# Layer 3's offsets and modulation: computed once per image and copied to all partitions through memory, for six of eight images

## The chip, the cores and the metric

The kernel runs on one core of one Trainium2 chip. The core has five engines that each run their own instruction stream in order and wait for one another by semaphores: TensorE (PE in the profile; its weight loads are PEld), VectorE (DVE), ScalarE (ACT), GpSimd (POOL) and SyncE (SP), which here only issues DMAs. Data live in HBM ("DRAM" in the code), in SBUF (128 partitions) and in PSUM, where TensorE writes its results. The metric is the device time of one execution in microseconds (us); lower is better.

## The reference

Eight images of 384 channels and 32x32 pixels in float32 pass four residual layers, each after a group norm. Layer 0 is a convolutional attention, layer 1 a mixture of four two-layer experts, layer 2 a ternary depthwise and pointwise convolution, layer 3 a deformable attention. The change lies in layer 3:

```python
q = einsum('bchw,oc->bohw', x, q_w)
q_off = q.reshape(B * 3, 128, H, W)                      # three groups
off = conv(q_off, dw_w, stride 2, pad 2, depthwise 5x5)  # 16x16 positions
off = gelu(batchnorm(off + dw_b))
om = einsum('bchw,oc->bohw', off, pw_w)                  # 3 numbers per position
offset, modulation = om[:, 0:2], sigmoid(om[:, 2:3])
pos = tanh(offset) * (2 / 16) + reference_points         # (y, x)
x_s = bilinear_sample(x, pos) * sigmoid(modulation)
k, v = kv_w @ x_s                                        # 256 keys per image
out = x + proj_w @ softmax(q k / 8) v + proj_b
```

So each image has 3 x 768 numbers `om`: for each of three groups and 256 positions a y offset, an x offset and a modulation. All channels of a group share them.

## The kernel before, in words

Layer 0 runs first over all images. Then layers 1, 2 and 3 run image by image. Layer 1 is cut into 48 *units* per image (`layer1`): 24 `hidden` units (six matmul records `ph` each, line L1244) and 24 `result` units (six records `y` each, L1265). In the main loop the layers 2 and 3 of image b (`layers(b)`, a generator) are written out together with the units of layer 1 of image b+1. The generator's `yield` gives a number, the idle time that TensorE is supposed to have there; the loop adds it to `due` and writes out one unit for every `UNIT = 2.6` of it. Units left over when the image ends are written out at the end. The last two images take another way: image 6 runs up to `yield None` with the units of image 7, and then its remainder is interleaved with image 7.

The framework orders each engine's instructions by this written order but puts later work that is ready ahead of work that isn't, by its own model of durations. So the order in the trace is near to the written one, not equal to it.

Around the change, layer 3 of an image does this:

- `pq`, `px` (L1384, L1407): q, and the transposed image `xT` which the sampling needs.
- `off` (L1452, L1454): the 5x5 convolution on VectorE, 25 taps; then Gelu on ScalarE (L1459).
- `pom` (L1467, L1468): three matmul pairs, one for each of y offset, x offset and modulation. The weight `pw3` in memory holds each of the three vectors repeated in 128 columns, so that the result of each pair stands in all 128 partitions at once. A Tanh (L1471) takes each pair from PSUM into the tile `om0`, `om1` or `om2`, each 128 x 768. The modulation's is scaled by 0.5, as a sigmoid is computed through a tanh.
- VectorE turns the offsets into pixel positions (L1477, L1481); ScalarE finishes the modulation (L1482; L1483 on VectorE) and the x weights (L1485, L1486); for each of eight row blocks ScalarE (L1499, L1500) and GpSimd (L1501) make the sampling weights `wt`, and TensorE samples with them (`xsb`, L1505).
- `xs` (L1512), `pk`, `pv` (L1519, L1528), attention (`s` L1545, `p` L1552, `pav` L1561, `pss` L1587), projection `pf` (L1650), output.

The pool `flat` has five buffers, `om0` to `om2` one each. SyncE's DMA queue carries, per image, three stores of layer 2's result (L1355), three loads of x (L171) and three of layer 0's output (L1179) for a later image, and three stores of the output (L1661).

```python
            for idle in this:
                ...
                due += idle
                while due >= UNIT and units:
                    units.pop(0)()
                    due -= UNIT
```

Of the kernel before, what the change touches and what calls it, by code (L numbers as in the profile page):

```python
# [7 lines left out]
F32 = mybir.dt.float32  # L8
AF = mybir.ActivationFunctionType
# [3 lines left out]
B, C, H, W = 8, 384, 32, 32  # L13
N = H * W
P = 128
# [17 lines left out]
NPAIR3, HS, LS, NG = 3, 16, 256, 3  # L33
# [19 lines left out]
def tile_kernel(ctx: ExitStack, tc: tile.TileContext, i: dict, out: bass.AP):  # L53
    nc = tc.nc
# [4 lines left out]
    dram = ctx.enter_context(tc.tile_pool(name="dram", bufs=1, space=bass.MemoryType.DRAM))  # L59
# [7 lines left out]
    def bank(name):  # L67
        return ps_mm.tile([P, HALF], F32, tag="mm", name=name)
# [150 lines left out]
    with ExitStack() as pa:  # L219
# [10 lines left out]
        for s in range(2):  # L230
            t = wa.tile([P, KC, H + 2, W], F32, name=f"pad{s}")
# [122 lines left out]
        for n, (b, g) in enumerate(work):  # L354
# [6 lines left out]
            if n in todo:  # L361
                f, b2 = todo.pop(n)
# [10 lines left out]
            for h, k in steps:  # L373
                dx, c0, c1, o0 = TAPS[k]
                rows = slice(h * (H // 2), (h + 1) * (H // 2))
                if g < NGC:
                    lhs, rhs = cw[:, g, dx, :], st[:, rows, c0:c1]
                else:
                    r = slice(32 * h, 32 * h + 3 * GR)
                    lhs, rhs = cwr[r, dx, :], st[r, rows, c0:c1]  # L380
                nc.tensor.matmul(  # L381
                    pk[h].rearrange("p (h w) -> p h w", w=W)[: 3 * nch, :, o0 : o0 + c1 - c0],
                    lhsT=lhs, rhs=rhs, start=(k == 0), stop=(k == 2),
# [31 lines left out]
        for v in range(3):  # L415
            nc.tensor.matmul(
                pm[:, 0, v, : 2 * (NGC + 1)], lhsT=sel0[:, v, :],
                rhs=both.rearrange("p s g -> p (s g)"), start=True, stop=True,
# [3 lines left out]
                rhs=rest.rearrange("p s k -> p (s k)"), start=True, stop=True,  # L422
# [28 lines left out]
    scale = HD0 ** (-0.5)  # L451
# [40 lines left out]
    with ExitStack() as pb:  # L492
# [17 lines left out]
        for v, nm in enumerate(("wq0", "wk0", "wv0")):  # L510
            t = wb.tile(list(i[nm].shape), F32, name=f"{nm}_sb")
# [225 lines left out]
    _, sco, sho = sc_o  # L737
# [51 lines left out]
    with tc.If(redo > 0):  # L789
        with ExitStack() as pb:  # L790
# [5 lines left out]
            for v, nm in enumerate(("wq0", "wk0", "wv0")):  # L796
                t = wb.tile(list(i[nm].shape), F32, name=f"{nm}_e")
# [6 lines left out]
            with tc.For_i(0, B) as bi:  # L804
                act = []
                for v in range(3):
                    g = work[v]
                    nc.sync.dma_start(
                        out=g, in_=raw[v][bass.ds(bi, 1)].rearrange("o p c n -> p (o c) n")
# [3 lines left out]
                for t in range(NT8):  # L813
                    pv = bank(f"pv_e{t}")
                    for c in range(KC):
                        nc.tensor.matmul(
                            pv[:, :C], lhsT=act[2][:, c, t * P : (t + 1) * P],
                            rhs=w_in[2][:, c, :], start=(c == 0), stop=(c == KC - 1),
# [8 lines left out]
                for v in range(2):  # L827
                    ts = qp.tile([P, NPAIR0, N], F32, tag=f"qk{v}", name=f"qk{v}_e")
                    for pr in range(KC):
                        for h in range(2):  # L830
                            pq = bank(f"pq{v}_e{pr}_{h}")
                            for c in range(KC):
                                nc.tensor.matmul(
                                    pq, lhsT=w_in[v][:, c, pr * P : (pr + 1) * P],
                                    rhs=act[v][:, c, h * HALF : (h + 1) * HALF],
                                    start=(c == 0), stop=(c == KC - 1),
# [8 lines left out]
                for pr in range(NPAIR0):  # L845
                    qt, kt = qks[0][:, pr, :], qks[1][:, pr, :]
                    for h in range(2):
                        pav = bank(f"pav_e{pr}_{h}")
                        for j, r in enumerate(HR):
                            hd = 2 * pr + j  # L850
                            pt = qp.tile([P, NT8, HALF], F32, tag="pt", name=f"pt_e{pr}_{h}_{j}")
                            for qc in range(4):
# [3 lines left out]
                                for kh in range(2):  # L856
# [3 lines left out]
                                        start=True, stop=True,  # L860
# [18 lines left out]
                            for kc in range(NT8):  # L879
                                nc.tensor.matmul(  # L880
                                    pav[64 * j : 64 * j + 64, :],
                                    lhsT=vt[:, kc, 2 * hd : 2 * hd + 2, :].rearrange(
                                        "p a b -> p (a b)"
                                    ),
                                    rhs=pt[:, kc, :],
                                    start=(kc == 0),
                                    stop=(kc == NT8 - 1),
# [5 lines left out]
                for m in range(KC):  # L893
                    for h in range(2):
                        hs = slice(h * HALF, (h + 1) * HALF)
                        po = bank(f"po_e{m}_{h}")
                        for c in range(KC):
                            nc.tensor.matmul(
                                po, lhsT=wo0[:, c, m * P : (m + 1) * P], rhs=att[:, c, hs],
                                start=(c == 0), stop=(c == KC - 1),  # L900
# [3 lines left out]
                    out=o_dram[bass.ds(bi, 1)].rearrange("o p c n -> p (o c) n"), in_=oe  # L904
# [19 lines left out]
    def load_w(name):  # L924
        src = i[name]
        t = wd.tile(list(src.shape), F32, tag=name, name=name + "_sb")
        nc.sync.dma_start(out=t, in_=src)
        return t
# [27 lines left out]
    pl = Pools(pd, "d")  # L956
# [190 lines left out]


    x2_dram = dram.tile([B, P, KC, N], F32, name="x2")
    NU3 = 2 * NPAIR3  # L1150
    rec3 = wd.tile([P, B * NU3, 16], F32, name="rec3")
    bad3 = wd.tile([P, 1], mybir.dt.int32, name="bad3")
# [205 lines left out]
    def layer3(pl, b, xt, put, general):  # L1358
# [14 lines left out]
        else:  # L1373
            t = pl.img(f"h3_{b}")
# [5 lines left out]
        for m in range(KC):  # L1380
            whole, pq = pair(last, f"pq3_{b}_{m}")
            for h in range(2):
                for c in range(KC):
                    nc.tensor.matmul(  # L1384
                        pq[h], lhsT=wq3[:, c, m * P : (m + 1) * P], rhs=h3[h][:, c, :],
                        start=(c == 0), stop=(c == KC - 1),
# [11 lines left out]
        else:  # L1398
            t = pl.img(f"xT_{b}").rearrange("p c n -> p (c n)")
# [38 lines left out]
        for t in (12, *range(12), *range(13, 25)):  # L1438
# [4 lines left out]
            for g in gs:  # L1443
                if g is None:
                    d = off.rearrange("p g h w -> p (g h) w")[:, :, c0 : c1 + 1]
                    f = q.rearrange("p g (h w) -> p (g h) w", h=H)[:, dy : : 2, :]
                else:
                    d = off[:, g, r0 : r1 + 1, c0 : c1 + 1]
                    f = src[:, g, 2 * r0 + dy : 2 * r1 + dy + 1 : 2, :]
                f = f[:, :, 2 * c0 + dx : 2 * c1 + dx + 1 : 2]  # L1450
# [7 lines left out]
        offf = off.rearrange("p g h w -> p (g h w)")  # L1458
# [3 lines left out]
        yield None  # L1462

        om = []
        for r in range(3):
            po = big(f"pom_{b}_{r}")
            nc.tensor.matmul(po[:, :512], lhsT=pw3[:, r, :], rhs=offf[:, :512], start=True, stop=True)  # L1467
            nc.tensor.matmul(po[:, 512:768], lhsT=pw3[:, r, :], rhs=offf[:, 512:], start=True, stop=True)  # L1468
            t = pl.one([P, NG * LS], f"om{r}", f"om{r}_{b}")

            nc.scalar.activation(t, po[:, : NG * LS], AF.Tanh, scale=1.0 if r < 2 else 0.5)  # L1471
            om.append(t)
            yield 0.3
# [21 lines left out]
        for t in range(NT8):  # L1495
# [8 lines left out]
            for g in range(NG):  # L1504
                nc.tensor.matmul(  # L1505
                    xps[g][:, sl], lhsT=xT[t // T2][:, t % T2, g * P : (g + 1) * P], rhs=wt[:, g, :],
                    start=False, stop=(t == NT8 - 1), skip_group_check=True,
# [9 lines left out]
        for m in range(NPAIR3):  # L1517
            for c in range(KC):
                nc.tensor.matmul(  # L1519
                    pk[:, m * LS : (m + 1) * LS], lhsT=wk3[:, c, m * P : (m + 1) * P],  # L1520
                    rhs=xs[:, c, :], start=(c == 0), stop=(c == KC - 1),
# [4 lines left out]
        for t in range(2):  # L1526
            for c in range(KC):
                nc.tensor.matmul(  # L1528
                    pv[:, t, :C], lhsT=xs[:, c, t * P : (t + 1) * P], rhs=wv3[:, c, :],
                    start=(c == 0), stop=(c == KC - 1),  # L1530
# [40 lines left out]
        if not general:  # L1571
            ps = scores(*units[0])
            for u, (pr, h) in enumerate(units):
# [5 lines left out]
                nc.vector.transpose(tu.rearrange("p a b -> p (a b)"), pav)  # L1579
                if u + 1 < NU3:  # L1580
                    ps = scores(*units[u + 1])
# [4 lines left out]
                for j in range(2):  # L1586
                    nc.tensor.matmul(  # L1587
                        pss[64 * j : 64 * j + 64, :], lhsT=ones[:, :64],
                        rhs=p01[:, j * HALF : (j + 1) * HALF], start=True, stop=True,
                    )  # L1590
                tss = blocks("ts")
                nc.vector.transpose(tss.rearrange("p a b -> p (a b)"), pss)
                rc = rec3[:, b * NU3 + u, :]
                nc.vector.reciprocal(rc, tss[:, :, 0])
# [8 lines left out]
        else:  # L1603
            for pr, h in units:
                pav = vbank(f"pav3_{b}_{pr}_{h}")
                for j in range(2):
                    r = slice(64 * j, 64 * j + 64)
                    nm = f"3_{b}_{pr}_{h}_{j}"
                    s = big(f"s{nm}").rearrange("p (a k) -> p a k", a=4)
                    for qc in range(4):  # L1610
# [3 lines left out]
                            start=True, stop=True,  # L1614
# [6 lines left out]
                    for qc in range(4):  # L1621
                        nc.scalar.activation(
                            p[:, qc, :], s[:, qc, :], AF.Exp, bias=mx[:, qc : qc + 1],
                            scale=0.125, accum_out=rs[:, qc : qc + 1],
# [14 lines left out]
                    for kc in range(2):  # L1639
                        nc.tensor.matmul(  # L1640
                            pav[r, :], lhsT=vt[:, kc, hd * 64 : (hd + 1) * 64], rhs=pt[:, kc, :],
                            start=(kc == 0), stop=(kc == 1),
                        )
                nc.vector.tensor_copy(att[:, pr, h * HALF : (h + 1) * HALF], pav)
        for m in range(KC):
            pf = big(f"pf_{b}_{m}")
            for h in range(2):
                hs = slice(h * HALF, (h + 1) * HALF)
                for pr in range(NPAIR3):
                    nc.tensor.matmul(  # L1650
                        pf[:, hs], lhsT=wp3[:, pr, m * P : (m + 1) * P], rhs=att[:, pr, hs],
                        start=(pr == 0), stop=(pr == NPAIR3 - 1),
# [16 lines left out]
    for b in range(1, B):  # L1669
        logits(b)  # L1670
        del fetched[b, 0]
        for n in (2, 3) if b == 1 else (b + 2,):
            if n < B:
                fetch_next(n)
        if b + 3 == B:
            w2, b2 = load_w("w2"), load_w("b2")
            wq3, wk3, wv3, wp3 = (load_w(n) for n in ("wq3", "wk3", "wv3", "wp3"))
            pb3, dw3, bn3, pw3 = (load_w(n) for n in ("pb3", "dw3", "bn3", "pw3"))
            ref3, npos = load_w("ref3"), load_w("npos")
        if b + 1 < B:  # L1680
            for _ in range(3 if b < 6 else 2):
                units.pop(0)()
    route(units, 2 * NE * KC)
    coefficients()
    with pd:
# [30 lines left out]
        for _ in following:  # L1716
            pass
        okt = pl.flat([P, B * NU3 * 16], "okt3")
        recf = rec3.rearrange("p u q -> p (u q)")
# [9 lines left out]
    with tc.If(redo3 > 0):  # L1729
        with ExitStack() as pe:  # L1730
            pl = Pools(pe, "g")
            with tc.For_i(0, B) as bi:
                xt = pl.img("x_g")
                nc.sync.dma_start(
                    out=xt, in_=x2_dram[bass.ds(bi, 1)].rearrange("o p c n -> p (o c) n")
# [28 lines left out]
def _layouts(a):  # L1764
    import numpy as np

    f = np.float32
    L = {}
# [53 lines left out]
    for n in "qk":  # L1822
# [27 lines left out]
    L["bn3"] = np.stack(  # L1850
        [a[f"L3_conv_{n}"] for n in ("dw_b", "bn_w", "bn_b", "bn_mean", "bn_var")], axis=1
    )
    L["pw3"] = np.repeat(a["L3_conv_pw_w"].T[:, :, None], P, axis=2)
    lin = np.linspace(0.5, HS - 0.5, HS, dtype=f) / f(HS) * f(2.0) - f(1.0)
    ref = np.stack([np.repeat(lin, HS), np.tile(lin, HS)])
# [26 lines left out]
```

## Time and profile before

| What | us |
|---|---|
| median of 3 runs (lowest to highest) | 3773.9 (3771.85 to 3775.54) |
| the profiled execution | 3772.12 |
| its span, first to last instruction | 3770.3 |
| TensorE busy in the span | 3647.7 |
| VectorE busy | 1818.9 |
| ScalarE busy | 1316.8 |
| GpSimd busy | 194.8 |
| one image of the main loop (from the end of one `pf` to the next, image 1) | 227.47 |
| TensorE busy in it | 226.00 |
| VectorE busy in it | 135.77 |

The busy times of the page are unions of intervals; a matmul's end is modelled, so TensorE's busy time says only that it had something in work. The distance between the starts of consecutive matmul records says what a record costs. Every float32 matmul of this kernel shows as two records.

### The profile page before, as it was taken

What the parts mean: (1) busy time and instruction counts of PE and PEld (TensorE: products, weight loads), DVE (VectorE), ACT (ScalarE), POOL (GpSimd) and SP (SyncE); (2) the same over time, 40 slices, a digit from 0 to 9 for tenths busy, and PEclk for the clock granted to TensorE, in tenths of its full rate; (3) what the DMA queues carried; (4) which work ended last, traced back from release to release, by engine and by line L of the source; (5) the groups of instructions that cost most, each with busy time, mean ns of one, the idle gap of its engine ahead of it and who ended that gap; (6) DMA issues with size and microseconds to landing.
All of it is one profiled execution on the core that took longest, in us unless ns stands there. A gap on an engine that the chain in (4) does not pass through costs nothing.

```text
span 3770.3 us, 39346 instructions
## 1 busy us (share of the span) xinstructions
PE 3647.7 (97%) x15754; PEld 1521.3 (40%) x15754; DVE 1818.9 (48%) x2841; ACT 1316.8 (35%) x1564; POOL 194.8 (5%) x153
## 2 busy tenths in 40 slices
PE   7999899999999999999799999999999999999898
PEld 3444333333333333333244534445444444444433
DVE  5876223232323232323346557565664666547664
ACT  2222364554545454534222321323222232322222
POOL 0000000000000000000000010200102010010111
PEclk9999999999999999999899999999999999999898
DMA  6777311111212020212340000100001001010000
GB/s 201 240 245 245 107 50 37 65 44 55 61 41 74 25 74 26 72 27 71 138 183 25 26 34 17 34 34 17 34 17 49 19 17 34 17 51 17 1 34 18
DMA packets 83097, 242.64 MB, mean 64 GB/s; under 512 B 18336, under 2 KB 18864, under 8 KB 82520
## 3 DMA queue, kind: packets, MB, share of 16 engines
q1 hardware_dynamic: 69894, 200.56, 16.1%
q10 hardware_dynamic: 13008, 39.43, 3.1%
q8 instruction: 128, 2.10, 0.2%
q14 instruction: 67, 0.55, 0.0%
HBM read 122.78 MB, written 75.50 MB: 53 GB/s over the span
## 4 chain that ended last, share of the span: by engine, by line
PE 40%; DVE 9%; ACT 1%; issue 0%; POOL 0%; DVEq 0%; POOLq 0%; ACTq 0%
PE y L1265 11%; PE ph L1244 8%; DVE y L1339 6%; PE pq L1384 3%; PE pw L1347 3%; PE pf L1650 3%; PE s L1545 3%; PE pav L1561 2%; PE pss L1587 1%; DVE hd L1230 1%; DVE off L1454 1%; PE pk L1519 1%; PE pv L1528 1%; PE xsb L1505 1%; PE plog L1007 1%; PE pom L1467 1%
## 5 line engine op out<-in xcount | busy, mean ns | idle before, releaser
L630 ACT ACTIVATE p<-s 128x1024 f32<-128x1024 f32 x512 | 496.4, 1021 | 496.9 <-PE s L623 496.5
L1265 PE MATMUL y<-hd,w_sb 128*128 128x512 f32 x1080 | 491.0, 600 | 3.6 <-DVE hd L1230 3.6
L638 PE MATMUL pav<-p,vt 64*64 64x512 f32 x4096 | 486.6, 590 | 0.0
L1244 PE MATMUL ph<-h,w_sb 128*128 128x512 f32 x1104 | 483.3, 594 | 0.0
L623 PE MATMUL s<-qk,qk 48*64 48x512 f32 x3072 | 372.7, 600 | 4.4 <-ACT p L630 4.4
L381 PE MATMUL pk<-st,cw_sb 126*126 126x512 f32 x720 | 316.4, 600 | 5.2 <-DVE ga_a L118 4.2
L1244 PEld LDWEIGHTS ph<-h,w_sb 128*128 128x128 f32 x1104 | 207.6, 190 | 253.1 <-issue 250.3
L1265 PEld LDWEIGHTS y<-hd,w_sb 128*128 128x128 f32 x1080 | 199.3, 191 | 249.8 <-issue 236.0
L638 PEld LDWEIGHTS pav<-p,vt 64*64 64x64 f32 x4096 | 156.2, 133 | 285.4 <-issue 285.1
L595 DVE COPY ta<-pav 128x512 f32<-128x512 f32 x64 | 44.3, 691 | 439.2 <-PE pav L638 439.2
L1339 DVE SCALAR_TENSOR_TENSOR y<-h,tap,y 128x992 f32<-128x992 f32 (+1 forms) x192 | 233.8, 1241 | 1.6
L1454 DVE SCALAR_TENSOR_TENSOR off<-q,dw_sb,off 128x225 f32<-128x225 f32 (+3 forms) x432 | 213.3, 549 | 1.7
L1254 ACT ACTIVATE hd<-ph,b_sb 128x512 f32<-128x512 f32 x180 | 122.7, 682 | 258.3 <-PE ph L1244 257.9
L381 PEld LDWEIGHTS pk<-st,cw_sb 126*126 126x126 f32 x720 | 137.6, 193 | 176.8 <-issue 167.8
L623 PEld LDWEIGHTS s<-qk,qk 48*64 48x64 f32 x3072 | 102.5, 132 | 241.5 <-issue 184.6
L78 DVE COPY qk<-pq 128x512 f32<-128x512 f32 x48 | 33.2, 691 | 293.6 <-PE pq L558 281.8
L387 ACT COPY y<-pk 126x512 f32<-126x512 f32 (+1 forms) x136 | 75.9, 584 | 250.7 <-PE pk L381 118.3
L1552 ACT ACTIVATE p<-s 128x1024 f32<-128x1024 f32 x96 | 93.1, 1021 | 173.4 <-PE s L1545 173.3
L575 PE MATMUL po<-att,wo_sb 128*128 128x512 f32 x288 | 135.7, 621 | 8.5 <-DMA att<-al 8.5
L1230 DVE TENSOR_TENSOR hd<-hd,cb 128x512 f32<-128x512 f32 x180 | 122.2, 684 | 35.4 <-ACT hd L1254 35.0
L1347 PE MATMUL pw<-y,upw 128*128 128x512 f32 x288 | 129.7, 603 | 7.6 <-DVE y L1339 7.6
L558 PE MATMUL pq<-g,wq_sb 128*128 128x512 f32 x288 | 132.8, 612 | 2.2 <-ACT g L483 2.2
(278 smaller groups left out, 4004.4 us busy)
## 6 DMA issues: line engine op xcount, KB each, us to landing
g<-raw SPq DMA_DIRECT2D x72, 512.0 KB
st<-pad SPq DMA_DIRECT2D x180, 168.0 KB
raw<-y ACTq DMA_DIRECT2D x180, 168.0 KB
xa<-in_x_dram SPq DMA_DIRECT2D x24, 512.0 KB
xh<-in_x_dram SPq DMA_DIRECT2D x48, 256.0 KB
f<-in_x_dram SPq DMA_DIRECT2D x24, 512.0 KB
f<-o SPq DMA_DIRECT2D x24, 512.0 KB
o<-ot SPq DMA_DIRECT2D x42, 256.0 KB
```

The source lines that it names most:

```text
L381: nc.tensor.matmul(pk[h].rearrange("p (h w) -> p h w", w=W)[: 3 * nch, :, o0 : o0 + c1 - c0], lhsT=lhs, rhs=rhs, start=(k == 0), stop=(k = ...
L558: nc.tensor.matmul(pq, lhsT=w_in[v][:, c, pr * P : (pr + 1) * P], rhs=acts[b][v][:, c, h * HALF : (h + 1) * HALF], start=(c == 0), stop=(c ...
L575: nc.tensor.matmul(po, lhsT=wo0[:, c, m * P : (m + 1) * P], rhs=atts[b][:, c, hs], start=(c == 0), stop=(c == KC - 1),)
L623: nc.tensor.matmul(s[64 * k : 64 * k + 64, j * HALF : (j + 1) * HALF], lhsT=kt[r, k0 : k0 + 64], rhs=qt[r, h * HALF : (h + 1) * HALF], sta ...
L630: nc.scalar.activation(p, s, AF.Exp, scale=scale)
L638: nc.tensor.matmul(pav[k][64 * j : 64 * j + 64, :], lhsT=vts[b % 2][r, kc, 2 * hd : 2 * hd + 2, :].rearrange("p a b -> p (a b)"), rhs=p[r, ...
L1230: nc.vector.tensor_tensor(hd, hd, state["cb"], ALU.mult)
L1244: nc.tensor.matmul(ph, lhsT=w1[:, e, c, dc * P : (dc + 1) * P], rhs=state["h1"][c], start=(c == 0), stop=(c == KC - 1),)
L1265: nc.tensor.matmul(y, lhsT=w2[:, e, dc, m * P : (m + 1) * P], rhs=state[h, k], start=(k == 0), stop=(k == NE * KC - 1),)
L1339: nc.vector.scalar_tensor_tensor(d, f, tap2[:, c, t : t + 1], d, ALU.mult, ALU.add)
L1347: nc.tensor.matmul(pw[h], lhsT=upw2[:, c, m * P : (m + 1) * P], rhs=y[c][:, hs], start=(c == 0), stop=(c == KC - 1),)
L1454: nc.vector.scalar_tensor_tensor(d, f, dw3[:, t : t + 1], d, ALU.mult, ALU.add)
```

## The change

For images 0 to 5 (`b < B - 2`) the three pairs of matmuls become one: the weight is `pw3[:, :, 0]`, three columns, so that the result has three partitions, one for each of y offset, x offset and modulation. One Tanh on those three partitions, with a per-partition scale from a small new constant `half3`, takes it into a `flat` tile. SyncE stores the three rows to a new DRAM tensor `om_dram` and loads each row back into all 128 partitions of `om0`, `om1` and `om2`. A single `yield 7.0` stands in place of three `yield 0.3`. Images 6 and 7, and the general path that is taken only when softmax sums leave their range, keep the three pairs. The constant `half3` is loaded with layer 3's other constants.

```diff
     x2_dram = dram.tile([B, P, KC, N], F32, name="x2")
+    om_dram = dram.tile([B, 3, NG * LS], F32, name="omd")
...
         om = []
-        for r in range(3):
+        if b < B - 2:
+
+            po = big(f"pom_{b}")
+            for k in (slice(0, 512), slice(512, 768)):
+                nc.tensor.matmul(po[:3, k], lhsT=pw3[:, :, 0], rhs=offf[:, k], start=True, stop=True)
+            t = pl.flat([P, NG * LS], f"oms_{b}")
+            nc.scalar.activation(t[:3], po[:3, : NG * LS], AF.Tanh, scale=half3)
+            nc.sync.dma_start(out=om_dram[b], in_=t[:3])
+            for r in range(3):
+                t = pl.one([P, NG * LS], f"om{r}", f"om{r}_{b}")
+                nc.sync.dma_start(out=t, in_=om_dram[b, r : r + 1].to_broadcast([P, NG * LS]))
+                om.append(t)
+            yield 7.0
+        for r in range(0 if om else 3):
             po = big(f"pom_{b}_{r}")
...
-            ref3, npos = load_w("ref3"), load_w("npos")
+            ref3, npos, half3 = load_w("ref3"), load_w("npos"), load_w("half3")
...
+    L["half3"] = np.array([[1.0], [1.0], [0.5]], f)
```

## The prediction

> **What bounds the kernel.** I read the page first, then the windows of one image, then TensorE's timeline around `pom` and at the image's end.
>
> ```profile
> PE 3647.7 (97%) x15754; PEld 1521.3 (40%) x15754; DVE 1818.9 (48%) x2841; ACT 1316.8 (35%) x1564; POOL 194.8 (5%) x153
> ```
>
> ```profile
> 2236.97:2464.44 227.47, 226.00 (x655) 102.10 (x655) 135.77 (x199) 62.51 (x85) 20.11 (x16) 1.00 0.08 28
> ```
>
> TensorE has work in 226.00 of an image's 227.47 us; it waits 1.5 us. So a TensorE microsecond removed from a main-loop image is one off the time, if the waits don't grow.
>
> ```profile
> 2141.76 1.02 PE L1467 MATMUL pom<-off,pw_sb 128*128 128x512 f32 x2
> 2142.62 0.59 PE L1468 MATMUL pom<-off,pw_sb 128*128 128x256 f32 x2
> 2143.05 1.02 PE L1467 MATMUL pom<-off,pw_sb 128*128 128x512 f32 x2
> 2143.91 0.59 PE L1468 MATMUL pom<-off,pw_sb 128*128 128x256 f32 x2
> 2144.34 1.02 PE L1467 MATMUL pom<-off,pw_sb 128*128 128x512 f32 x2
> 2145.20 0.59 PE L1468 MATMUL pom<-off,pw_sb 128*128 128x256 f32 x2
> 2145.63 5.31 PE L1244 MATMUL ph<-h,w_sb 128*128 128x512 f32 x12
> 2150.78 2.74 PE L1265 MATMUL y<-hd,w_sb 128*128 128x512 f32 x6
> 2153.35 0.54 PE L1505 MATMUL xsb<-wt,xT 128*128 128x48 f32 x4
> ```
>
> No bracket at a line's end means no wait. Starts give the cost: a pair takes 1.29 us (2141.76 to 2143.05), a unit six records of 0.43, 2.58 us. TensorE runs three units (12 `ph`, 6 `y`) between `pom` and the sampling. What the sampling waits for:
>
> ```profile
> 2143.25 0.81 ACT L1471 ACTIVATE om<-pom 128x768 f32<-128x768 f32 x1 [0.60 <-PE pom L1468]
> 2146.91 0.92 ACT L1482 ACTIVATE om<-om,quarter 128x768 f32<-128x768 f32 x1
> 2147.73 0.92 ACT L1485 ACTIVATE om<-om,npos_sb 128x768 f32<-128x768 f32 x1
> 2148.90 0.83 ACT L1486 ACTIVATE om<-om 128x768 f32<-128x768 f32 x1
> 2149.81 0.49 POOL L1501 TENSOR_TENSOR wt<-wt,om 128x144 f32<-128x144 f32 x1 [68.23 <-ACT om L1486]
> ```
>
> The first `wt` is there at 2150.30, TensorE comes to it at 2153.35: 3 us of slack today.
>
> **What the Trainium skill says.** "TensorE: Matmul & The Clock Gate", Back-to-back issue gap: the gap follows the streamed columns N. So three output rows cost what 128 do per streamed column; the trace agrees, as `pk` with 18x18 weights has 574 ns beside 579 ns with 126x126 (modelled ends, so weak). "DMA: Bandwidth & Descriptors", Two DMAs through the same engine are not ordered: a DMA that reads what another wrote must be issued after a semaphore wait. So SyncE waits for the store before it issues the loads; no DMA pair of that kind near `pom` shows it before. Two prices are below.
>
> **The change part by part.** Clock: t = 0 at the start of `pom`.
>
> *Removed.* Two pairs per image: 2 x 1.29 = 2.58 us of TensorE, on the path. Six images: 15.5 us. Two Tanhs (0.81 us each) leave ScalarE, which is busy 62.5 of 227 us: worth nothing; it is covered by TensorE's work and has slack without it.
>
> *Added: the trip through memory.* Tanh starts at 1.49 as now (2143.25 less 2141.76) and ends at 2.30; ScalarE's cost here goes by the row's 768 elements, which stay. Then store and loads. SyncE is free there: in image 1 it issues its stores from 2295.5 to 2305.3 and the next load at 2389.28, while `pom` starts at 2369.57. Queued behind the four DMAs is only that load of x, whose data are wanted an image later: cost nothing.
>
> The store (9 KB): no row shows one. The page's Anatomy of one DMA section prices a transfer at about 2.0 us plus bytes/436e3, for the GpSimd path; the estimate is 2.0 (bounds 1.5 to 3.0). It lands at 4.4, with 0.1 for semaphores.
>
> The loads (384 KB each): the nearest row is layer 0's output, 512 KB from memory. SyncE issues the first at 2008.68, and VectorE, waiting for it, starts at 2012.32: 3.64 us. The DMA view of image 1 shows 280 GB/s while x is loaded (from 2389), at which 512 KB take 1.87; the fixed part is 1.77. A load of 384 KB takes 1.40 more, and the three share the same DMA engines: `om0` at 4.4 + 1.77 + 1.40 = 7.6, `om1` 9.0, `om2` 10.4. What is new is that 128 reads fetch the same 3 KB. Low bound 0.9 us each (435 GB/s, the page's ceiling): `om2` 8.9. High bound: Latency and other measured facts gives 103 GB/s where streams fall on the same memory channels, 3.8 us each: `om2` 17.6. I take the middle, as the reads are whole rows.
>
> From L1482, which wants `om2`, to the first `wt` today: 2150.30 - 2146.91 = 3.39. VectorE's work on `om1` (0.96 + 0.56) is done at about 10.6, so ScalarE's order keeps this distance: `wt` at 10.4 + 3.4 = 13.8.
>
> *Moved: the cover.* The ledger of yields for a whole image adds up to 118.55; at 2.6 that is 45 of 48 units, three left over. The trace agrees:
>
> ```profile
> 2221.35 15.61 PE L1650 MATMUL pf<-att,wp_sb 128*128 128x512 f32 x36
> 2236.80 7.89 PE L1265 MATMUL y<-hd,w_sb 128*128 128x512 f32 x18
> 2244.53 1.05 PE L1208 MATMUL w<-ident_sb,w 128*128 128x128 f32 x8
> ```
>
> With 7.0 for 0.9 the sum is 124.65, 47 units, one left. Between `pom` and the sampling the yields add up to 7.0 + 6.0 + 2.0 = 15.0 in place of 0.9 + 6.0 + 2.0 = 8.9: stepping the ledger from the image's start writes six units there in place of four. One of them runs ahead of `pom` today, while `pom` waits for Gelu (ten `ph` units stand before `pom`, nine by the ledger); so five remain in place of the three seen. TensorE reaches the sampling at 1.29 + 5 x 2.58 = 14.2, just after `wt` at 13.8. GpSimd's fourth block follows 2.95 later (2153.25 less 2150.30), at 16.8; TensorE wants it at 14.2 + 3 x 0.65 = 16.1, unless a unit lies between. So I count a wait of 0.5 us per image (0 to 0.7). A unit written earlier costs TensorE nothing: the two units leave the end of the image, where they kept TensorE busy after `pf`; there the next image's `ph` follow, whose inputs are ready at 2219.9, well before. VectorE's chain from the last `y` to layer 2's pointwise product starts earlier by what TensorE saves and keeps its length; TensorE waits 0.67 for it at 2290.47 today, and will again.
>
> *VectorE and ScalarE wait in order.* L1477 waits for `om0`; behind it are the `hd` products (L1230) of the two `ph` units, which the second `y` group needs. Both `ph` are done by 6.5, before `om0`, so the products mostly go ahead. If not, three units of `y` don't need them.
>
> *Buffers and constants.* The new `flat` tile lives from 1.5 to 4.4, when one more of five (`off`) is held: nothing waits. `half3` is one more tiny load among fourteen issued from 1912 to 1926: nothing.
>
> Sum: 6 x (-2.58 + 0.5) = -12.5. The profiled execution, 3772.12 with its span of 3770.3, becomes 3759.6; the median lies 1.8 above it, so 3761.4.
>
> **The rivals.**
>
> *The loads are late (slower).* Place: the wait of ScalarE's L1482 and VectorE's L1477 on the loads; TensorE then stands at `xsb`, because order is fixed and no further unit fills. Each microsecond of `om2` after 10.8 costs one per image. It decides at 10.8 + 2.58 = 13.4, where the gain is gone: 3.0 us per load in place of my 1.4, wherever the row is read at under about 160 GB/s (393 KB by 2.4 us, the store as priced). At the high bound `om2` 17.6 gives `wt` at 21.0, a wait of 6.8, net +4.2 per image, +25: 3799. For it: no row in the profile reads one row 128 times. Against it: DMA is at 0.00 of its capacity in this stretch, and the framework can place more `y` there if its model expects long DMAs, as 12 units remain.
>
> *The wait takes most of the gain (no change).* Store plus loads 2 us slower than priced: wait 2 to 2.5, net -0.5 x 6 = -3: 3771.
>
> *More gain.* All lands in time and the moved units also close the 0.55 wait before `pav`: 6 x -2.9 = -17: 3757. Little speaks for it; those waits have units near already.
>
> *It does not do what it says*: if the three-column matmul cost more than a pair of 128 columns. Weights of three columns load no slower; I give it no chance of its own.
>
> **How the numbers follow.** A measurement of this kernel tells about 0.2%, 7.5 us, from no change. In time or a wait up to 1.3 us: 0.50 (predicted; 3756 to 3766 of itself). Wait of 1.3 to 3.8: 0.18. Later: 0.32, of which about half past 3795. With half of them reached and the early end kept, the range is 3755 to 3798; some 0.16 lie above and 0.02 below.
>
> **What would show it.** Two `pom` pairs fewer on TensorE's timeline and `ph` 1.29 after `pom`. The image period: 227.3 less 2.1, about 225.3. The wait of PE `xsb` L1505 on POOL `wt`: absent before, up to 0.7 per image after; over 2.6 the forecast is wrong. Waits of L1477 and L1482 on DMA, and the distance from the store's issue to them, price the trip. After `pf`, 6 `y` records, not 18. The forecast also falls if the framework places `xsb` so early that TensorE stands before it, or if image 6 and 7, not changed, get another order.

## The result and the profile after

| | before | after |
|---|---|---|
| median of four runs (lowest to highest), us | 3772.88 (3765.86 to 3775.54) | 3756.68 (3755.51 to 3758.4) |
| ratio, with its 95% interval | | 0.996 (0.9943 to 0.9978) |
| the profiled execution, us | 3772.12 | 3756.19 |
| its span, us | 3770.3 | 3754.4 |

The change makes the kernel faster by 16.2 us (0.4%). The forecast was 3761.4 with a range of 3755 to 3798: right in direction and within the range, the time 4.7 us lower than foretold. (1.0 us of that is the base: the forecast started from 3773.9, the median of three runs, and the fourth brought it to 3772.88.) Three terms behind it were not what the prediction said.

The page of the kernel after, its line of busy times (engine, busy us, share, instructions):

```profile
PE 3631.3 (97%) x15706; PEld 1507.2 (40%) x15706; DVE 1820.7 (48%) x2841; ACT 1309.6 (35%) x1552; POOL 191.3 (5%) x153
```

TensorE is still busy 97% of the span and is 16.4 us less busy; 48 of its records are gone, which is 6 images x 2 pairs x 4 records. The same stretch of image 1 as was shown before, from the end of one `pf` to the end of the next (window, its length, and then the busy time of PE, PEld, DVE, ACT and POOL, the clock, the DMA share and GB/s):

```profile
2239.40:2463.73 224.33, 222.88 (x648) 99.64 (x646) 135.93 (x199) 61.29 (x83) 19.50 (x16) 1.00 0.09 34
```

The image takes 224.33 in place of 227.47 us, and TensorE's idle remainder is 1.45 as before (1.47). The whole gain of this image is TensorE work that takes less time; no wait came or went in it. TensorE's timeline from `pom` to the sampling, in image 0 as in the lines before the change (start, duration, engine, line, out<-in, weights, tile, records):

```profile
2142.78 1.46 PE L1470 MATMUL pom<-off,pw_sb 128*3 128x512 f32 x4
2144.17 5.42 PE L1245 MATMUL ph<-h,w_sb 128*128 128x512 f32 x12
2149.42 7.89 PE L1266 MATMUL y<-hd,w_sb 128*128 128x512 f32 x18
2157.14 0.54 PE L1519 MATMUL xsb<-wt,xT 128*128 128x48 f32 x4
```

One pair is left. Between it and `xsb` stand 12 `ph` and 18 `y` records, five units where there were three, and no bracket: TensorE doesn't wait for the trip. One pair now takes 1.39 us (2142.78 to 2144.17), not 1.29, and twelve `ph` take 5.25, not 5.15. The trip itself, in three views of the same stretch: SyncE's queue (`omd` is the DRAM tensor `om_dram`, `oms` the tile that is stored), the waiting engines, and the DMA view between 2130 and 2180 in bins of 1.25 us.

```profile
2145.19 0.26 SPq L1473 DMA_DIRECT2D omd<-oms  x1
2146.75 1.27 SPq L1476 DMA_DIRECT2D om<-omd  x3
```

```profile
2144.27 0.89 ACT L1472 ACTIVATE oms<-pom,half_sb 3x768 f32<-3x768 f32 x1 [0.70 <-PE pom L1470]
...
2150.95 0.95 DVE L1491 SCALAR_TENSOR_TENSOR om<-om,ref_sb 128x768 f32<-128x768 f32 x1
...
2153.41 0.92 ACT L1496 ACTIVATE om<-om,quarter 128x768 f32<-128x768 f32 x1
...
2156.22 2.14 POOL L1515 TENSOR_TENSOR wt<-wt,om 128x144 f32<-128x144 f32 x4 [73.69 <-ACT om L1500]
```

```profile
GB/s 0 0 0 0 0 0 0 7 0 0 0 0 7 0 182 300 396 66 0 0 0 0 0 0 0 0 0 0 0 0 0 197 383 419 249 20 3 0 0 0
```

SyncE issues the loads 1.56 us after the store. The bins 182, 300, 396 and 66 hold 1.18 MB (944 GB/s x 1.25 us), which is three loads of 384 KB; at the two full bins' mean rate of 348 GB/s they move from about 2148.1 to 2151.5. The second hump, up to 419, is the load of x. VectorE takes `om0` at 2150.95, right behind an `hd` product, and ScalarE takes `om2` at 2153.41, both without waiting for a DMA. GpSimd starts the four first `wt` blocks 13.44 us after `pom`; the first is ready at about 13.9 (0.5 us later, as one took before), and TensorE arrives at 14.36: the cover holds with 0.4 us to spare.

The end of image 0, on the same timeline:

```profile
2223.95 15.61 PE L1664 MATMUL pf<-att,wp_sb 128*128 128x512 f32 x36
2239.40 2.74 PE L1266 MATMUL y<-hd,w_sb 128*128 128x512 f32 x6
```

One unit is left after `pf`, not three.

**Where the 15.9 us of the span are.** I cut each trace at TensorE's first `pw` record of an image. From the first image's to the seventh's, so over the six changed images, the distance is 1364.13 before and 1344.98 after: -19.15. What lies ahead of it is 0.95 longer, and what lies behind it (images 6 and 7 and the general path) 2.28 longer: 3770.3 - 19.15 + 0.95 + 2.28 = 3754.4. This distance is a steady measure where the total is not: in all twelve profiled executions of this document TensorE's granted clock is 1.00 over it, and two executions of the change give 1344.98 and 1345.03. Ahead of it, where these kernels differ by no more than the load of a small constant, the clock is 0.98 and the stretch takes anything from 2055.9 to 2068.8 us. In the comparisons below, "the six images" is this distance in the profiled execution. Within an image I sum, for each product, the distances from the start of each of its records to the next record of TensorE, whatever that is, so that the sums of all products add up to the image. Between the two kernels they differ, in image 1, in these:

```
us in image 1     before   after
pom                 3.87    1.39
s                  14.82   13.77
ph                 61.97   62.17
y                  64.20   64.46
xsb                 3.45    3.39
all others          equal within 0.01
```

Only the first line was in the forecast. The second is a gain nobody asked for, the third and fourth are costs.

### The profile page after: what moved, and what is told of

Its sections match the earlier page's. It is cut to its first block, busy times and chain, and to the rows that moved or that the text cites. A ratio compares the mean times of both kernels' runs of the same rounds, so it can differ in the third digit from the quotient of the medians.

```text
span 3754.4 us, 39254 instructions
## 1 busy us (share of the span) xinstructions
PE 3631.3 (97%) x15706; PEld 1507.2 (40%) x15706; DVE 1820.7 (48%) x2841; ACT 1309.6 (35%) x1552; POOL 191.3 (5%) x153
```

## The experiments

Three accounts fit the total. The two pairs give the gain, and the rest is chance. Or the new order of the units gives it. Or the trip costs something on other engines that the order makes good. My theory, by the sums of image 1: the pairs give most of it, the shorter `s` comes from the new places of the `result` units, and the trip itself is hidden.

**The yields alone.** Three pairs in 128 partitions as before, no trip; only the ledger as in the change.

```diff
-            yield 0.3
+            yield 6.4 if r == 2 and b < B - 2 else 0.3
```

> The kernel before with the yields of the change alone: the third pair of images 0 to 5 yields 6.4 in place of 0.3, so two units of layer 1 move from behind the projection to ahead of the sampling. All three pairs stay, nothing goes through memory. Theory (the gain is the two pairs of matmuls): TensorE has the same work, so at most the 1.1 to 1.4 us per image that the attention's waits shrank by comes back: 3766 to 3773. Rival (the gain is the new order of units): most of the 16 us, 3757 to 3761.

Measured: 3771.73 (3767.54 to 3773.74), ratio 0.9992 (0.9984 to 1.0). The six images: 1358.79, 5.34 less. `s` is at 13.77 as in the change, `pom` and `ph` at 3.87 and 61.97 as before. So the order of the units is worth 5.3 us by itself, though the total scarcely shows it, as the profiled execution took 3.1 us longer ahead of the six images and 2.2 behind them (more on that below).

**One pair alone.** The pairs of the x offset and of the modulation are left out for six images (their Tanhs read the first pair's result); no trip, yields as before.

```diff
+            if r == 0 or b >= B - 2:
                 nc.tensor.matmul(...)
```

> The kernel before with the second and third pair of matmuls left out for images 0 to 5; all three Tanhs read the first pair's result, so offsets and modulation are the same numbers and the sampling is at other places. Yields and all else as before, nothing goes through memory. Theory: 2.1 to 2.5 us per image go, 3757 to 3761. Rival (order of units): no change, 3770 to 3774.

Measured: 3759.94 (3754.56 to 3769.3), ratio 0.9967 (0.9954 to 0.9981). The six images: 1348.81, 15.32 less. The forecast's 15.5 is confirmed to 0.2.

**One pair with the yields.** Both edits together, the same computation left out: the change without its trip.

> As the run with one pair (the second and third pair left out for images 0 to 5, their numbers taken from the first), and with the yields of the change. That is the change without the trip through memory. Theory (the trip is hidden): the same as the changed kernel, 3754 to 3759. Rival (the trip costs some, and the gain without it would be larger): 3745 to 3752.

Measured: 3754.5 (3748.04 to 3757.61), ratio 0.9948 (0.9936 to 0.996). The six images: 1343.27, 20.86 less; the sum of the two single edits is 20.66.

**The trip with three pairs.** The change with its product written out three times, so that TensorE does the old amount of work.

```diff
-            for k in (slice(0, 512), slice(512, 768)):
+            for k in (slice(0, 512), slice(512, 768)) * 3:
```

> The changed kernel with its pair of three-column matmuls run three times into the same place for images 0 to 5; trip through memory and yields as changed. Theory: 2 x 1.29 us of TensorE per image come back, 3771 to 3773, or a few us less where the attention's waits stay shorter. Rival (order of units): stays at 3757.

Measured: 3771.71 (3767.66 to 3777.04), ratio 0.9995 (0.9987 to 1.0003). The six images: 1360.43, so 1.64 more than with the yields alone. `pom` is 3.96 and `ph` 62.17: the same 0.1 and 0.2 us more per image as in the change, though the product stands there three times. So the cost does not grow with the records of the product; it lies at its two borders, and TensorE's weight loads (PEld) show it. Before, and then in the change, at the borders of `pom`:

```profile
2141.33 0.19 PEld L1467 LDWEIGHTS pom<-off,pw_sb 128*128 128x128 f32 x1 [0.24 <-issue]
```

```profile
2142.78 0.09 PEld L1470 LDWEIGHTS pom<-off,pw_sb 128*3 128x3 f32 x2 [0.76 <-ACT hd L1255]
2144.16 0.30 PEld L1245 LDWEIGHTS ph<-h,w_sb 128*128 128x128 f32 x2 [0.44 <-issue]
```

Before, the first load starts at 2141.33 for a product that starts at 2141.76, one record ahead, while the last `ph` record still runs. In the change the loads at both borders start only with their own products (2142.78 and 2144.17). The load of three columns is itself the shorter one, 0.09 for 0.19 us. Three records take 0.1 us longer for it: the last `ph` before the product (0.52 for 0.43), the product's last (0.31 for 0.22), and the first `ph` behind it (0.53 for 0.43).

**A short yield.** The change with 0.9 in place of 7.0, so that the ledger asks for no cover.

```diff
-            yield 7.0
+            yield 0.9
```

> The changed kernel with a yield of 0.9 in place of 7.0, the sum that the three yields of before had. Theory (what covers the trip is that TensorE has other work that is ready, and the framework moves it ahead by itself): five units still stand between the pair and the sampling, but four sampling blocks follow at once, so up to 0.7 us of wait per image and the attention's waits of before: 3757 to 3766. Rival (the 7.0 is what hides the trip): three units as before, a wait of 5 us less the 2.6 saved, 3770 to 3790.

Measured: 3761.44 (3758.35 to 3767.77), ratio 0.9963 (0.9949 to 0.9977). The six images: 1350.42. TensorE doesn't wait at the sampling here either: the framework still puts two `ph` and three `y` units ahead of it, and though six sampling blocks follow one another here without a unit between, none of them waits. So the cover at the sampling doesn't rest on the `yield 7.0`. But `s` is back at 14.81.

These five and the two kernels form a table of three edits. Every edit is worth the same within 0.2 us, whatever it stands beside:

```
                       trip, 3 columns, yields    no trip, yields    trip, no yields    no trip, no yields
three pairs                   1360.43                1358.79                -                1364.13
one pair                      1344.98                1343.27             1350.42            1348.81

pairs:   1344.98-1360.43 = -15.45   1343.27-1358.79 = -15.52   1348.81-1364.13 = -15.32
yields:  1344.98-1350.42 =  -5.44   1343.27-1348.81 =  -5.54   1358.79-1364.13 =  -5.34
trip:    1344.98-1343.27 =  +1.71   1350.42-1348.81 =  +1.61   1360.43-1358.79 =  +1.64
```

(All six images. "yields" is 7.0 in place of 0.9 behind `pom`; the trip and the three columns always stand together.) The rivals fall: the rest beyond the pairs comes again to 0.2 us in each pairing, the order is a third of what the pairs are, and the trip costs the same with and without the new order.

**What the yields do.** TensorE's timeline in the attention of image 1, before and after:

```profile
2407.62 1.99 PE L1545 MATMUL s<-q,kt 64*128 64x512 f32 x8
2409.54 1.08 PE L1587 MATMUL pss<-p,ones 128*64 128x512 f32 x4
2410.55 1.12 PE L1545 MATMUL s<-q,kt 64*128 64x512 f32 x2
2411.60 1.94 PE L1561 MATMUL pav<-p,vt 128*64 128x512 f32 x8
2413.47 1.98 PE L1545 MATMUL s<-q,kt 64*128 64x512 f32 x6
2415.56 1.08 PE L1587 MATMUL pss<-p,ones 128*64 128x512 f32 x4
```

```profile
2407.93 1.99 PE L1559 MATMUL s<-q,kt 64*128 64x512 f32 x8
2409.84 1.08 PE L1601 MATMUL pss<-p,ones 128*64 128x512 f32 x4
2410.85 1.98 PE L1266 MATMUL y<-hd,w_sb 128*128 128x512 f32 x4
2412.77 1.94 PE L1575 MATMUL pav<-p,vt 128*64 128x512 f32 x8
2414.64 1.99 PE L1559 MATMUL s<-q,kt 64*128 64x512 f32 x8
2416.55 1.08 PE L1601 MATMUL pss<-p,ones 128*64 128x512 f32 x4
```

The scores of one step are eight records. Together they take 1.91 us (2414.64 to 2416.55), and the records start two by two at the same time: each of the two heads uses 64 of the 128 rows. Where the framework puts no `y` behind `pss`, it takes two of the eight ahead of `pav` to fill the place (why it has no `y` for it, the traces don't say). These two are of one head and run one after the other, 1.05 us (2410.55 to 2411.60); the six left behind take 2.09 (0.1 of it a wait) and 1.91, no less than eight. So each group that is split costs 1.05 us more. In the main loop's images the kernel before splits three of six groups, the change two. In the seven kernels of the table the count goes with the yields without exception: with the old, three splits in each of the six images and `s` at 14.81 or 14.82, in image 0 15.16 or 15.17; with the new, two splits and 13.76 to 13.78. That is -1.05 in each image and 0.35 more in image 0, where `s` lost a wait; +0.26 for `y` goes against it, most of it at borders again: six `y` records take 2.77 us between `pss` and `pav`, whose weights have 64 columns, and 2.58 between products of 128, and the attention has seven groups of `y` for six. Together: 6 x (-1.05 + 0.26 - 0.06) - 0.35 = -5.45, with the -0.06 of `xsb` (5.44 measured in the change).

**Two hops.** Is there slack in the trip? The store goes to a second tensor first, and a copy within memory brings it to `om_dram`.

```diff
-            nc.sync.dma_start(out=om_dram[b], in_=t[:3])
+            nc.sync.dma_start(out=om_hop[b], in_=t[:3])
+            nc.sync.dma_start(out=om_dram[b], in_=om_hop[b])
```

> The changed kernel with a second trip: the three rows are stored to one DRAM tensor, copied to a second one by a DMA, and loaded from there. About 1.5 to 2 us more from Tanh to landing. Theory: covered, as further units of layer 1 are ready and one more is put ahead of the sampling: no change to the changed kernel, 3754 to 3760. Rival (the trip is at its limit): 1.5 us per image, 3764 to 3769.

Measured: 3759.32 (3754.02 to 3762.29), ratio 0.9957 (0.9943 to 0.997). The six images: 1345.08, 0.1 more than the change. SyncE's queue in image 1, and TensorE's line that ends at the sampling:

```profile
2373.23 0.26 SPq L1474 DMA_DIRECT2D omh<-oms  x1
2374.66 0.52 SPq L1475 DMA_DIRECT2D omd<-omh  x1
2376.82 1.49 SPq L1478 DMA_DIRECT2D om<-omd  x3
```

```profile
2377.45 10.46 PE L1267 MATMUL y<-hd,w_sb 128*128 128x512 f32 x24
```

The loads are issued 3.59 us after the store, 2.15 later than in the change (1.44 in image 1), and TensorE still doesn't wait: the framework puts a fourth `y` unit ahead of the sampling, 24 records in place of 18. This is the forecast's sentence that the framework can place more `y` there, seen at work.

**All eight images.** Images 6 and 7 take the trip too.

```diff
-        if b < B - 2:
+        if not general:
```

> The change for all eight images. In the last two there are no units of layer 1 to cover the trip; in image 7 TensorE waits 4.4 us for the first sampling weights as it is. Theory: the trip's 3.5 to 6 us come on top there, less nothing for the pairs, which weren't on that path: 3759 to 3766. Rival (the trip is short enough anyway): 3750 to 3757.

Measured: 3763.66 (3760.11 to 3768.64), ratio 0.9973 (0.9962 to 0.9984). The six images: 1345.03, as in the change; what lies behind them is 6.5 us longer (355.44 against 348.91, and 345.83 in a second run of the change, below). Image 7 has no units of a next image, and so shows the trip bare:

```profile
3667.51 0.26 SPq L1473 DMA_DIRECT2D omd<-oms  x1
3668.98 1.29 SPq L1476 DMA_DIRECT2D om<-omd  x3
...
3672.67 0.96 DVE L1491 SCALAR_TENSOR_TENSOR om<-om,ref_sb 128x768 f32<-128x768 f32 x1 [9.29 <-DMA om<-omd]
...
3678.48 1.09 PE L1519 MATMUL xsb<-wt,xT 128*128 128x48 f32 x4 [11.99 <-POOL wt L1515]
```

The store has landed after 1.47 us, the first load 3.69 after its issue: `om0` is there 5.2 us after the Tanh's end (3667.48). TensorE waits 11.99 us for the sampling weights; in the change, where this image keeps its three pairs, it waits 4.40. In image 6 the wait is 12.09 in place of 7.94. Together that is 11.7 us more wait at the sampling, about 6 per image, against two images' pairs. This is the rival of the late loads, in the place where there is no cover. The sum is not clean: `pom` of image 7 waits 11.35 us for Gelu in place of 6.68, and the granted clock is 0.50 for 37.5 us around that image's sampling, in place of two stretches of 20.5 in all. What of the 6.5 us is the trip alone stays open; that it costs more than it saves there is what the run shows.

**Packed.** The three groups of 256 positions go to partitions 0, 32 and 64 of PSUM as three products of 256 columns, with one Tanh of three partitions and one store each.

```diff
-            for k in (slice(0, 512), slice(512, 768)):
-                nc.tensor.matmul(po[:3, k], lhsT=pw3[:, :, 0], rhs=offf[:, k], start=True, stop=True)
+            for g in range(NG):
+                nc.tensor.matmul(po[32 * g : 32 * g + 3, :LS], lhsT=pw3[:, :, 0],
+                                 rhs=offf[:, g * LS : (g + 1) * LS], start=True, stop=True)
...
```

> The changed kernel with the pair cut into three matmuls of 256 columns, one per group, whose three rows go to partitions 0, 32 and 64 of one PSUM place; Tanh and store go three times, on 256 columns each. Theory: if matmuls whose results lie in different quarters of the partitions overlap, as the 64-row ones of the attention seem to (0.24 us per record of 512 columns in place of 0.43), 0.9 us of TensorE go per image and the longer store is covered: 3750 to 3754. Rival (no overlap, or the three stores are late): 3756 to 3765.

Measured: 3750.25 (3744.67 to 3753.89), ratio 0.9937 (0.9923 to 0.9951). The six images: 1340.22. TensorE's timeline in image 0:

```profile
2138.63 0.61 PE L1470 MATMUL pom<-off,pw_sb 128*3 128x256 f32 x6
2139.17 5.42 PE L1245 MATMUL ph<-h,w_sb 128*128 128x512 f32 x12
```

The whole product takes 0.54 us (2138.63 to 2139.17) in place of 1.39: the three groups run beside each other. The product accounts for 6 x 0.85 = 5.1 us less than in the change; 4.8 remain, as in image 3 `pss` waits 0.40 us where it waits 0.10 in the others. The three Tanhs of 0.46 us and three stores lie in the cover.

**Packed, with a longer yield, and the change again.** One more unit asked for behind `pom` in the packed kernel (9.6 for 7.0); beside it the change as it is, on one chip.

> The packed kernel with 9.6 us in place of 7.0 us of units asked for behind the offsets, so that one more `y` unit stands ahead of the sampling. If the gain of the order comes from `y` units left for the attention, whose small waits they fill, a unit moved ahead of the sampling leaves fewer for the attention: image periods within 0.2 us of the packed kernel's, 1340 to 1342 us for the six, and 3749 to 3755 us. If the order's gain comes from units standing behind the offsets as such, it grows by another 0.3 to 0.9 us per image, 1335 to 1338 us for the six, and 3744 to 3749 us.

> The change as it is, beside the packed kernels on one chip. The six periods should come again at 1345 us within 0.5, 4.8 us above the packed kernel's, and the time at 3755 to 3760 us. If the stretch at half rate in the general path's attention belongs to this kernel, it shows again and the last two images take 348.9 us from the first `pw` of the seventh on; if it is a matter of the single execution, they take 346.5 us as in the kernel before.

Measured: packed with 9.6, 3756.44 (3752.11 to 3758.03), ratio 0.9952 (0.9939 to 0.9966), six images 1342.14, 1.92 more than packed with 7.0. The change again: 3756.59 (3753.43 to 3760.41), ratio 0.9955 (0.9942 to 0.9969), six images 1345.03 (1344.98 in the first). The order's gain does not grow with the units asked for; it turns. The split count stays at two, but a wait comes back in the attention of image 1:

```profile
2417.00 1.08 PE L1606 MATMUL pss<-p,ones 128*64 128x512 f32 x4 [0.39 <-DVE tu L1598]
```

`s`, in which this wait is counted, takes 14.06 in place of 13.77 in all six images, where the packed kernel has it in one; in image 1, and only there, `ph` takes 0.19 more. I expected a loss of at most 0.2 us per image; it is 0.3. The median lies 1.4 above the upper of the two ranges, and 6.2 over the packed kernel's own, more than the 1.9 of the six images. The two profiled executions, 7.4 us apart, show where such a rest comes from: 2.9 ahead of the six images and 2.6 behind them, where the two kernels don't differ.

By the medians the packed kernel is the fastest that computes everything, 6.3 us under the change; but its interval, 0.9923 to 0.9951, and the change's, 0.9942 to 0.9969, overlap. What carries the gain is the record of the six images, 4.8 us less, with the product's own 0.54 us.

**The end of the span.** From the first `pw` of the seventh image on, with the last two images unchanged, the kernels take either 345.8 to 347.5 us (before, and six of the experiments, the change's second run among them with 345.83) or 348.8 to 348.9 (the change's first run, yields alone, two hops, packed with 9.6). In the four long ones, and in none of the seven short ones, a whole group of records in the attention of image 6 runs at half rate. (The text on record for the change's second run calls this place the general path's; it is not.) The change's first run and its second, with the granted clock of the stretch (the third number from the end of the second line):

```profile
3628.91 3.68 PE L1575 MATMUL pav<-p,vt 128*64 128x512 f32 x8
3628.91:3632.60 3.69, 3.69 (x11) 0.85 (x10) 0.45 (x2) 0.00 (x0) 0.00 (x0) 0.50 0.00 0
```

```profile
3631.08 1.94 PE L1575 MATMUL pav<-p,vt 128*64 128x512 f32 x8
3631.08:3633.02 1.94, 1.94 (x11) 0.56 (x10) 1.83 (x4) 0.00 (x0) 0.00 (x0) 1.00 0.00 0
```

The half rate is the granted clock, 0.50 in the first stretch and 1.00 in the second. At this place it is 0.50 for 6.8 us in the four long kernels, for 3.4 us in five of the short ones (346.6 to 347.5), and not at all in the other two (345.8 and 346.3). The same kernel shows it once and not once. So the 2.28 us that the change's profile lost at its end are a matter of the single execution and not of the change. What makes the clock fall in one execution and not in the other stays open: in both TensorE has waited 2.85 us for `xT` 3 to 5 us earlier, so that wait alone doesn't decide it, and no run here varied it.

## Why the prediction was right, and where not

The main term and the cover were right. That the total came so near is in part luck: the six images missed the forecast by 3.0 us for a wait that didn't come, by 5.4 for the order and by 1.7 the other way for the product's form, and the profiled execution gave 3.2 of that back at its two ends by chance.

- **The removed pairs** (2 x 1.29 per image, 15.5 in all): right. One pair alone gave 15.32, and the two other pairings 15.45 and 15.52.
- **The counted wait of 0.5 per image at `xsb`** (+3.0 in all): wrong, it is 0. `wt` and TensorE's arrival stood as worked out (13.8 foretold for the first block, about 13.9 measured; 14.2 and 14.36 for TensorE). What failed is the step that took the fourth block 2.95 us after the first, from the kernel before. There ScalarE made the later blocks' parts between two `hd` activations. Now these are over before `om0` comes (they start at 2147.05 and 2149.62), and the four blocks follow without a gap: 2.14 for four, ready at 15.6 where 16.8 was reckoned. In the run with the short yield, where the blocks follow one another on TensorE, the fourth was wanted at 16.3 and was there at 15.6; in the change a `y` unit stands behind the second block besides.
- **The trip.** The store was priced at 2.0 and took 1.44 to 1.56 in the main loop and 1.47 bare, from its issue to that of the loads; the 2.0 came from the Trainium skill, "DMA: Bandwidth & Descriptors", Anatomy of one DMA, which prices GpSimd's path, and SyncE's was quicker here. The loads were put at 1.40 each, with a bound of 3.8 for 128 reads of the same 3 KB; they move at up to 396 GB/s, and 1.18 MB in some 3.4 us makes about 1.1 us each, near the low bound of 0.9. (The 103 GB/s behind the high bound, in the same page's Latency and other measured facts, belong there to copies whose rows lie 4 or 8 MiB apart, and shared channels are given as an inference; the one row read here is another form, and its rate was far above that. And the prediction's "3.0 us per load", where the gain would be gone, counts the fixed part in: with 1.77 taken off first it is 2.4, the figure that its 160 GB/s rests on.) The fixed part came out longer: 3.69 less 1.1 is 2.6 for the bare trip, where I had 1.77. These errors cancel, and `om0` was 5.2 after the Tanh's end for 5.3 reckoned. ScalarE's L1496 had `om2` 10.6 after `pom` starts at the latest, for 10.4. The Tanh on 3 partitions took 0.89 us, no less than the 0.81 on 128. Right in sum, with two terms mis-sized.
- **The moved units**, five ahead of the sampling and one left behind `pf`: right. "A unit written earlier costs TensorE nothing": wrong on the good side. What the step left out is that the places of the `y` units in the attention decide whether a group of scores is split, 1.05 us each; the change has one split less per image, and the yields' whole worth is -5.4 over six images.
- **"Weights of three columns load no slower", so the pair costs the same**: wrong by 0.3 us per image, 1.7 in all. The loads are no slower, and within the product a record costs what it did (0.43 and 0.22 us). What the step left out is the border: the load isn't taken ahead there. `pom` is 0.1 longer in every kernel with one or three three-column pairs, `ph` 0.2 in every kernel with the three-column product, the packed ones too, and neither in any without. The section of the Trainium skill that the prediction leans on, "TensorE: Matmul & The Clock Gate", Back-to-back issue gap, gives the gap by N for a single product, and says ahead of it that in a stream of loads and products both set the spacing; the prediction passed over this half, and the 0.3 us lie there. Whether the weights' form or the output's three partitions keep the load back, no run separates.
- **VectorE's chain to `pw`**: right, TensorE waits 0.66 there, for 0.67 foretold. Two Tanhs less, the queue on SyncE, the new tile: worth nothing, as said; the three-pair kernel with the trip loses the 1.64 us of the product's form and no more.
- **The image period**: 225.3 foretold, 224.33 and 223.99 in turn measured (227.36 before, as a mean). Sum over six images: -12.5 foretold; pairs -15.4, wait 0, order -5.4, product's form +1.7 make -19.1, measured -19.15.
- **The rivals of the prediction.** The rival "more gain" (3757) named the size but a wrong cause: the wait of 0.55 before `pav` is still 0.55. The late loads don't come about in the six images; they do in the two without cover: with all eight images the median is 7 us above the change's, and what lies behind the six images 6.5 us longer. That the framework stretches the cover by itself was given as a reason against it, and the two hops show it.

## What to carry to other kernels

A product whose result is the same in all partitions can be done once and fetched from memory, if the engine that bounds the kernel has enough other work to run in between. Here the first sampling weights were ready 13.9 us after `pom` started, in place of 8.5, so five more microseconds had to be covered; without cover the trip cost more than it saved, as the last two images show. Where two half-height matmuls run side by side, count how often the order of instructions breaks up their group: here it was worth a third of the main gain, and moved with a number in the ledger that seemed to be about something else. A product with few output rows is worth a try in pieces that stand in different partitions: here three such pieces ran beside each other.

## What the runs showed that I had not expected

- Three products with three output partitions each, at partitions 0, 32 and 64, take 0.54 us together (six records), where two with all columns take 1.39.
- 128 partitions that read one 3 KB row of memory get it at up to 396 GB/s, close to the 419 of an ordinary load of x in the same view.
- Eight score records of two heads take 1.91 us, two of one head 1.05, and the six that are left behind 1.91, or 2.09 with a wait in it.
- Going from products with 128 columns to one with three and back costs 0.3 us per image, beside its own records: at each border the weight load starts with its product and not one record (0.43 us) ahead.
- A group of matmuls of some 2 us ran at half rate (3.68 for 1.94 us, at a granted clock of 0.50) in four of the profiled executions, and for the same kernel in one and not in the other.
